# Earlier accumulator loads, GpSimd weight loads, a place for the counts and early Gelus in a graph and FFN kernel

## The chip, the cores and the metric

The kernel runs on one core of a Trainium2 chip. The metric is the device time of one launch in microseconds; of several runs the median is taken. TensorE (PE) does the matmuls, VectorE (DVE) elementwise work, ScalarE (ACT) activations and copies, GpSimd (POOL) some elementwise work and DMA issue, and SyncE (SP) only issues DMAs. Each engine works through its own instructions in a fixed order.

## The reference, cut to what matters

All data are fp32. `x` has 1250 rows (nodes) of 1024. There are 20,000 edges (`src`, `dst`).

```python
x = x + gat(LN(x))           # graph attention, 4 heads of 256
x = x + ffn(LN(x))           # 4 x 64 rails of 16, up to 64 each, gelu, then 16384 -> 1024 by w_cproj
x = x + gcn(LN(x), W, b)     # h = LN(x) @ W.T + b, weighted sum over neighbours and self
x = x + moe(LN(x))           # shared geglu + one of 8 experts by argmax
```

The change touches the end of the attention, the FFN and the GCN. The FFN is

```python
y = einsum('btri,hrij->bthrj', xr, rail_maker)
z = einsum('bthrj,hrkj->bthrk', y, rail_up_proj)
out = gelu(z.reshape(b, t, -1)) @ w_cproj.T
```

and the GCN sums `norm[:, None] * h[col]` over the rows, for which the kernel uses a matrix of edge counts between nodes.

## The kernel before, in words

**Attention.** `attend(h, b)` does one head and half of the rows: DVE makes `u` (L434), ACT its Exp (L435), DVE the weights `w` (L438), PE multiplies (L440). At the end ACT copies row sums (L444), DVE inverts them (L446, L447) and adds the result to `X` (L450). While `attend(2, 1)` and `attend(3, 1)` run, `first_half` normalizes and transposes the first five tiles of 125 rows into `xT`. Tiles 0 to 4 of `X` are stored to DRAM (`x_d`) in between, and tiles 5 to 9 after the last `attend`.

**Blocks.** The FFN's projection is a Strassen multiplication within a Strassen multiplication. The hidden columns are in 16 blocks. A block has 7 outer products of 7 inner products each: 49 steps of eight matmuls (`product`, L583). The factors X (weights, 128x512) and Y (hidden values after Gelu, 128x626) live in 33 X places and 38 Y places, which are parts of tiles named `BZ`, `arena`, `X` (its memory, once the rows have gone to DRAM) and `low`. DVE adds up factors (`add_up`, L576); `projection_plan` lists these sums with a step by which each is due, planned about 11 us ahead of its product. `load_weights` fetches weights on SP's queue (L406) as X places come free. `hidden` makes the hidden values: four matmuls of a 32-row slice (L564) and two Gelus of 626 columns (L569). For block 0 it is called at steps 0 (two pieces), 2, 3, 7, 8, 9 and 10; for later blocks in the block before.

After each product of the blocks 0 to 14, ACT copies it from PSUM (L592) to one of five staging buffers in `low`, and GpSimd issues a DMA that adds it to an accumulator in DRAM, `acc_d[p, i]` (L596), 49 in all. Products have two places in PSUM.

**Last block.** Block 15 has 7 outer products of 4 steps, each step with two pairs of factors (16 matmuls). Before it, the accumulators come back: `load_sums(p)` (L611, SP) fetches the seven of outer product p, `outer_sums(p)` is a generator of seven DVE sums (L618) that make four blocks of it. `combine` adds a product in PSUM to its block (L632) and, for the later p, adds blocks to the output in `xT` (L637). With `end` the number of the first step of the last block, `load_sums` is called for p = 1, 2, 6, 7, 4, 5, 3 at steps end-7, end, end+4, end+8, end+12, end+16, end+20. From step end-4 on, two of the waiting L618 sums are written per step, and seven at every fourth step of the last block. The rest is in the order in which the program is written; the scheduler may move an instruction in front of others on its engine where nothing forbids it.

As the last block's X places come free, the 16 GCN weight pieces (`gcn_w`, 256 KB each) are loaded into them on SP (L736), from the fifteenth of its steps in the program on (the scheduler moves them forward).

**GCN.** `linear(t)` does tile t: 16 matmuls (L762), a bias by DVE (L769), a scale by ACT. Then, in a loop over r, SP loads 125 x 1250 counts (L823, which is two DMAs by the helper at L105 and L106) into one of three buffers of a pool, GpSimd adds the identity to one part (L824), and PE multiplies: 20 matmuls of 512 columns (L828). Before this loop, SP's queue has the loads of the shared expert's weights (L794 to L796) and of the gate, which go to the memory that the linear stage leaves.

Of the kernel before, what the change touches and what calls it, by code (L numbers as in the profile page):

```python
# [8 lines left out]
F32 = mybir.dt.float32  # L9
# [4 lines left out]
AF = mybir.ActivationFunctionType  # L14
ALU = mybir.AluOpType
# [4 lines left out]
P = 128  # L20
R, T = 125, 10
N = R * T
# [75 lines left out]
def gnn_ffn_kernel(ctx, tc, x, src, dst, gat_w, a_l, a_r, maker, up, cproj,  # L98
# [4 lines left out]
    def dma(eng, out, in_):  # L103

        eng.dma_start(out[:RA], in_[:RA])  # L105
        eng.dma_start(out[RA:], in_[RA:])  # L106
# [301 lines left out]
    def rail_parts(k):  # L408
        return (spare[:, k * 464 + i:k * 464 + j] for i, j in ((0, 16), (16, 80), (80, 208), (208, 336), (336, 464)))
# [10 lines left out]
    def rails(k, pp):  # L420
# [2 lines left out]
        nc.tensor.matmul(pp, mb, ub, start=True, stop=True)  # L423
        nc.scalar.copy(pw, pp)

    with tc.tile_pool(name="att", bufs=3) as atp, tc.tile_pool(name="aps", bufs=6, space=PSUM) as aps, \
            tc.tile_pool(name="tps0", bufs=2, space=PSUM) as tps:

# [40 lines left out]
        with tc.tile_pool(name="al", bufs=2) as lnp:  # L469
            attend(2, 0)  # L470
            nc.gpsimd.memset(m8, 1.0)
            nc.gpsimd.affine_select(m8, m8, pattern=[[-16, 8]], compare_op=ALU.is_ge, fill=0.0, base=0,
                                    channel_multiplier=1)
            nc.gpsimd.affine_select(m8, m8, pattern=[[16, 8]], compare_op=ALU.is_ge, fill=0.0, base=15,
                                    channel_multiplier=-1)
            nc.vector.tensor_reduce(m2, m8.rearrange("p (a s) -> p s a", s=2), AX.X, ALU.add)
            for k in range(2):
                load_rails(0, k)
            for o in ("11", "12"):
                for i in corner:  # L480
                    load_weights(0, o, i)
            end = attend(3, 0)
            with tc.issue_after(end.ins):
                for k in range(2):
                    rails(k, tps.tile([P, 4, R], F32, name="pt").rearrange("p a b -> p (a b)")[:, :P])
            for t in range(HT):
                dma(nc.sync, x_d[t], X[:, t, :])

            def first_half():
                mv = lnp.tile([R, HT, 2], F32, name="mvh", bufs=1)  # L490
                for t in range(HT):
                    st = lnp.tile([R, 2, 6], F32, name="st")
                    for g in range(2):
                        nc.vector.bn_stats(st[:, g, :], X[:, t, g * 512:(g + 1) * 512])
                    nc.vector.bn_aggr(mv[:, t, :], st.rearrange("p a b -> p (a b)"))
                    yield
                rstd = lnp.tile([R, HT], F32, name="rstdh", bufs=1)
                nc.scalar.activation(rstd, mv[:, :, 1], AF.Sqrt, bias=eps)
                nc.vector.reciprocal(rstd, rstd)
                for t in range(HT):  # L500
                    norm[t] = lnp.tile([R, D], F32, name="xn")
                    nc.vector.tensor_scalar(norm[t], X[:, t, :], mv[:, t, 0:1], rstd[:, t:t + 1],
                                            op0=ALU.subtract, op1=ALU.mult)
                    turn(xT, norm, tps, t)
                    yield

            half = first_half()
            attend(2, 1, half)
            attend(3, 1, half)
            for t in range(HT, T):  # L510
                dma(nc.sync, x_d[t], X[:, t, :])
    rowst.close()
# [8 lines left out]

    xx = XX.rearrange("p t d -> p (t d)")
    with ExitStack() as tail:
        low = tail.enter_context(tc.tile_pool(name="lowp", bufs=1)).tile([P, T * D], F32, name="low")
        Hs = low[:R].rearrange("p (t d) -> p t d", d=D)
        accst, blocks = ExitStack(), ExitStack()
        arena = accst.enter_context(tc.tile_pool(name="accp", bufs=1)).tile([P, 33 * 512], F32, name="arena")
        rlp = blocks.enter_context(tc.tile_pool(name="rl", bufs=2))  # L530
        ops = accst.enter_context(tc.tile_pool(name="ops", bufs=2, space=PSUM))
        zps = blocks.enter_context(tc.tile_pool(name="zps", bufs=1, space=PSUM))
        two = lambda a: a.rearrange("p (q n) -> p q n", q=2)

        scratch = arena[:, 25 * 512:]
        XS += [two(arena[:, i * 512:(i + 1) * 512]) for i in range(33)]
        xw += range(8, 33)
        YS = [two(v[:, i * 2 * NQ:(i + 1) * 2 * NQ]) for v, n in ((xx, 16), (low, 16), (scratch, 6)) for i in range(n)]
        yh, parts, early = [*range(8), *range(16, 27), *range(8, 16)], list(range(27, 32)), list(range(32, 38))
        tt = nc.vector.tensor_tensor  # L540
        steps, sums = projection_plan()
        left, acc = {}, {}
# [14 lines left out]

        def hidden(b, n, k):

            pw = [*rail_parts(k)][-1]  # L560
            pz = zps.tile([P, 4, 512], F32, name="pz2")
            for q in range(4):
                rows = slice(32 * q, 32 * q + 32)
                nc.tensor.matmul(pz[:, q, :NQ], pw[rows, :], xT[rows, (2 * b + k) % KD, n * NQ:(n + 1) * NQ],  # L564
                                 start=True, stop=True)
            for i in range(2):
                key = b, "Y", f"{k + 1}{n // 2 + 1}", f"{i + 1}{n % 2 + 1}"
                buf[key] = place_y(b == NB - 1 and n > 1)
                nc.scalar.activation(view(key), pz[:, 2 * i:2 * i + 2, :NQ], AF.Gelu)  # L569
# [104 lines left out]
        def turn_tile(t):  # L674
# [4 lines left out]
        coming = {b: list(raw) for b in range(1, NB)}  # L679
        coming[0] = raw[8:]  # L680
        pieces = [(n, k) for h in range(2) for k in range(2) for n in (2 * h, 2 * h + 1)]
        first = {0: pieces[:2], 2: pieces[2:3], 3: pieces[3:4], 7: pieces[4:5], 8: pieces[5:6], 9: pieces[6:7],
                 10: pieces[7:]}
        later = dict(zip((33, 36, 38, 40, 42, 44, 46, 48), pieces))
        late = {1: 5, 2: 6, 3: 7, 4: 8, 5: 9}
        end = (NB - 1) * 49
        last, j, fill, sums_of = None, 0, [], dict(zip((end - 7, *range(end, end + 21, 4)), OUTER))
        norm = {}
        for n, (b, p, i, pairs) in enumerate(steps):
            m = n - 49 * b  # L690
# [22 lines left out]
            if b + 1 < NB:  # L713
# [4 lines left out]
                    rails(m // 2 - 14, zps.tile([P, 4, 512], F32, name="pz2")[:, 0, :P])  # L718
                if m in later:
                    hidden(b + 1, *later[m])  # L720
            assert n != end - 7 or all(v < 33 for k, v in buf.items() if k[1] == "X")
            if n in sums_of:
                load_sums(sums_of[n])
                fill.append(outer_sums(sums_of[n]))
# [5 lines left out]
            if b == NB - 1:  # L730
                if m >= 14 and len(W3) < 2 * KD:
                    for g in range(2):
                        for k in range(KD):
                            if xw and (k, g) not in W3:
                                W3[k, g] = XS[xw.pop(0)].rearrange("p q o -> p (q o)")
                                nc.sync.dma_start(W3[k, g], gcn_w[k * P:(k + 1) * P, g * 512:(g + 1) * 512])  # L736
                if m == 23:
                    nc.gpsimd.dma_start(bias, gcn_b.partition_broadcast(R))
                while m >= 16 and len(fetched) < 4 and fetch(len(fetched)):
                    pass  # L740
                if m == 22:
                    add_out(0)
                    level(0)
                if m == 24:
                    turn_tile(0)
                if m == 27:
                    add_out(1)
                    level(1)
            po = product(pairs)
            for _ in range(7 if n >= end and m % 4 == 3 else 2):  # L750
                if n > end - 5 and fill and next(fill[0], 0) == 0:
                    fill.pop(0)
            if last:
                (combine if last[0] == NB - 1 else accumulate)(*last[last[0] == NB - 1:])
# [3 lines left out]
        def linear(t):  # L758
# [10 lines left out]
            tt(Hs[:, t, :], ph.rearrange("p a b -> p (a b)"), bias, op=ALU.add)  # L769
            nc.scalar.activation(Hs[:, t, :], Hs[:, t, :], AF.Copy, scale=dis[:, t:t + 1])  # L770

        for t in range(T):
            for w in range(len(fetched), min(T, t + 5)):
                fetch(w)
            linear(t)
# [3 lines left out]

        back_end = ExitStack()  # L780
        xTp = back_end.enter_context(tc.tile_pool(name="xp3", bufs=1, side="right"))
        cp = tail.enter_context(tc.tile_pool(name="cp", bufs=3))
        psp = tail.enter_context(tc.tile_pool(name="ps3", bufs=2, space=PSUM))

        keep = back_end.enter_context(tc.tile_pool(name="xp5", bufs=1, side="right"))
# [33 lines left out]
                nc.tensor.transpose(pl[:, t0 + i, :], lgT[:, i * R:(i + 1) * R], ident[:NE, :NE])  # L819

        for r in range(T):
            cs = cp.tile([R, T, R], F32, name="cs")
            dma(nc.sync, cs, cnt_d[r])  # L823
            nc.gpsimd.tensor_tensor(cs[:, r, :], cs[:, r, :], ident[:R, :R], op=ALU.add)  # L824
            pa = psp.tile([R, 2, 512], F32, name="ph")
            for c in range(T):
                for g in range(2):
                    nc.tensor.matmul(pa[:, g, :], cs[:, c, :], Hs[:, c, g * 512:(g + 1) * 512],  # L828
                                     start=(c == 0), stop=(c == T - 1))
            if r:  # L830
                turn(xT5, norm, psp, r - 1)
                if r in (5, 9):
                    logits(r - 5, 4)
            xs = X[:, r, :]
            nc.vector.scalar_tensor_tensor(xs, pa.rearrange("p a b -> p (a b)"), dis[:, r:r + 1], xs,
                                           op0=ALU.mult, op1=ALU.add)
            normalize(norm, lnp, r)
            dma(nc.sync, xn_d[r * R:(r + 1) * R, :], norm[r])
# [218 lines left out]
```

## Time and profile before

| | |
|---|---|
| median of 3 runs | 3000.86 us (3000.56 to 3002.55) |
| the profiled execution | 3001.98 us |
| its span | 3000.2 us, so 1.8 us lie around it |
| granted PE clock, mean | 0.987 |
| PE busy | 2903.7 us (97%) |
| DVE, ACT, GpSimd busy | 1595.9, 875.9, 753.9 us |
| DMA moved | 449.57 MB, 150 GB/s over the span |
| attention's last matmul ends | 502.43 us |
| blocks 0 to 14 and the last one | until about 2336 us |
| linear stage of the GCN | about 2336 to 2490 us |
| counts rounds | about 2503 to 2706 us |

The profile page gives busy times of each engine and groups of equal instructions. The list of waits names for each engine what it stood still for: engine, tile and line that waited, an arrow, what released it, then the total, the number of times and the longest. A stretch is a window of time with busy time (and number) of each engine in it, the clock that the throttle granted PE and the share of time in which DMA engines were busy. The chain of waits goes back from the end of a stretch: start, length and what the work was. The engine names with a q (SPq) are the instruction queues that issue.

### The profile page before, as it was taken

The page shows a single profiled execution, that of the slowest core. Times are in us where ns is not written, and L with a number is a line of the kernel's source. Part 1 is how long each engine was busy: PE and PEld are TensorE (multiplying, and loading weights), DVE is VectorE, ACT ScalarE, POOL GpSimd, SP SyncE. Part 2 cuts the span into 40 slices and gives each one's busy share as a digit, 9 for nine tenths or more (in the row PEclk, how much of TensorE's full clock was granted, in tenths as well). Part 3 has the DMA queues.
Part 4 walks back from the last instruction along what each step waited for, and adds up shares of the span by engine and source line. Part 5 has one row for each costly group of instructions (what it writes and reads, how often), then busy time and mean ns, then how long its engine had stood idle before and what let it go on. Part 6 is the DMA issues. An engine that isn't in the chain of part 4 may idle for free.

```text
span 3000.2 us, 32450 instructions
## 1 busy us (share of the span) xinstructions
PE 2903.7 (97%) x11479; PEld 1915.7 (64%) x11479; DVE 1595.9 (53%) x2611; ACT 875.9 (29%) x1412; POOL 753.9 (25%) x966
## 2 busy tenths in 40 slices
PE   8999898999999999999999999999979998999998
PEld 5574776666766766766766766766657543445774
DVE  7687987746645645645655555555557321221213
ACT  1211234444344344344344334334310110000000
POOL 2010000224434434434434434434310000002001
PEclk9999999999999999999999999999989998999999
DMA  5245523569999999999999999999974003212655
GB/s 140 64 119 146 142 65 122 186 166 173 196 172 172 195 177 167 196 178 166 195 181 163 198 179 162 200 178 144 232 195 132 25 0 98 61 58 82 211 195 161
DMA packets 253572, 449.57 MB, mean 150 GB/s; under 512 B 48160, under 2 KB 132218, under 8 KB 252777
## 3 DMA queue, kind: packets, MB, share of 16 engines
q0 software_dynamic: 113936, 266.34, 51.6%
q1 hardware_dynamic: 139466, 181.05, 20.1%
q8 instruction: 96, 1.57, 0.2%
q14 instruction: 74, 0.61, 0.1%
HBM read 175.38 MB, written 271.89 MB: 149 GB/s over the span
## 4 chain that ended last, share of the span: by engine, by line
PE 83%; DMA 2%; DVE 2%; ACT 0%; issue 0%; SPq 0%; POOL 0%; DVEq 0%; POOLq 0%; ACTq 0%
PE po L583 56%; PE ph L828 6%; PE pab L859 6%; PE po L762 5%; PE pz L564 3%; PE po L440 3%; PE po L965 2%; PE po L976 1%; PE pt L153 1%; DMA X<-acc_d 1%; PE pg L814 1%; DMA cs<-cnt_d 0%; DMA yg<-ys_d,back 0%; DMA rowbd<-st 0%; PE px L668 0%; DVE y L968 0%
## 5 line engine op out<-in xcount | busy, mean ns | idle before, releaser
L583 PE MATMUL po<-X,arena 128*128 128x313 f32 x3000 | 837.1, 429 | 0.0
L596 POOL DMA_DIRECT2D acc_d<-low x686 | 593.2, 865 | 914.4 <-ACT low L592 886.3
L592 ACT COPY low<-po 128x626 f32<-128x626 f32 x735 | 500.4, 681 | 993.1 <-PE po L583 820.8
L583 PEld LDWEIGHTS po<-X,arena 128*128 128x128 f32 x3000 | 563.3, 190 | 237.1 <-issue 26.3
L583 PE MATMUL po<-low,arena 128*128 128x313 f32 x2112 | 593.9, 429 | 16.1 <-DVE arena L632 16.1
L583 PEld LDWEIGHTS po<-low,arena 128*128 128x128 f32 x2112 | 396.7, 190 | 183.3 <-issue 18.7
L576 DVE TENSOR_TENSOR arena<-arena 128x512 f32<-128x512 f32 x339 | 233.3, 691 | 84.9 <-PE po L583 80.3
L583 PE MATMUL po<-X,BZ 128*128 128x313 f32 x736 | 213.2, 432 | 4.7 <-ACT X L569 4.7
L828 PE MATMUL ph<-low,cs 125*125 125x512 f32 x400 | 176.5, 601 | 14.5 <-POOL cs L824 14.5
L583 PEld LDWEIGHTS po<-X,BZ 128*128 128x128 f32 x736 | 139.0, 191 | 64.7 <-issue 8.3
L576 DVE TENSOR_TENSOR X<-X 128x626 f32<-128x626 f32 x137 | 111.2, 814 | 100.7 <-PE po L583 100.4
L828 PEld LDWEIGHTS ph<-low,cs 125*125 125x125 f32 x400 | 75.4, 191 | 109.7 <-issue 94.4
L209 PE MATMUL pz<-W,xT 128*125 128x512 f32 x320 | 141.2, 596 | 0.1
L583 PE MATMUL po<-low,BZ 128*128 128x313 f32 x480 | 138.3, 428 | 0.0
L576 DVE TENSOR_TENSOR X<-low,X 128x626 f32<-128x626 f32 x105 | 85.2, 816 | 85.2 <-PE po L583 82.6
L576 DVE TENSOR_TENSOR low<-X 128x626 f32<-128x626 f32 x103 | 83.7, 815 | 71.6 <-PE po L583 71.3
L576 DVE TENSOR_TENSOR X<-X,low 128x626 f32<-128x626 f32 x93 | 76.0, 819 | 79.9 <-PE po L583 79.7
L277 PE MATMUL pc<-os,od 125*125 125x417 f16 (+1 forms) x588 | 110.9, 344 | 5.1 <-issue 5.1
L440 PE MATMUL po<-BZ,w 125*125 125x257 f32 x400 | 98.2, 407 | 17.0 <-DVE w L438 15.7
L583 PEld LDWEIGHTS po<-low,BZ 128*128 128x128 f32 x480 | 90.0, 190 | 36.7 <-issue 3.0
L564 PE MATMUL pz<-xT,BZ 32*128 32x313 f32 x1024 | 104.9, 479 | 4.2 <-DVE X L450 4.2
L209 PEld LDWEIGHTS pz<-W,xT 128*125 128x125 f32 x320 | 59.0, 188 | 72.9 <-issue 70.0
(235 smaller groups left out, 2904.6 us busy)
## 6 DMA issues: line engine op xcount, KB each, us to landing
acc_d<-low POOLq DMA_DIRECT2D x735, 313.0 KB, 5.8
arena<-in_cproj SPq DMA_DIRECT2D x200, 256.0 KB
w<-in_w SPq DMA_DIRECT2D x16, 1024.0 KB
BZ<-in_cproj SPq DMA_DIRECT2D x56, 256.0 KB
nm<-nm_d SPq DMA_DIRECT2D x20, 546.9 KB
w3t<-in_w SPq DMA_DIRECT2D x8, 1024.0 KB
X<-acc_d SPq DMA_DIRECT2D x19, 313.0 KB
cnt_d<-cn SPq DMA_DIRECT2D x10, 546.9 KB
```

What stands on the lines that cost most here:

```text
L209: nc.tensor.matmul(pz, xT[:, k, t * R:(t + 1) * R], W[g][:, k], start=(k == 0), stop=(k == KD - 1))
L277: nc.tensor.matmul(pc[:, b, :nn], od[:, d - near[c][0], :], os[:, n0:n0 + nn], start=(c == win[d][0]), stop=(c == win[d][-1]))
L440: nc.tensor.matmul(po[i], w[:, i * R:(i + 1) * R], Z[h // 2][:, s, h % 2, :], start=(s == 0), stop=(s == T - 1))
L564: nc.tensor.matmul(pz[:, q, :NQ], pw[rows, :], xT[rows, (2 * b + k) % KD, n * NQ:(n + 1) * NQ], start=True, stop=True)
L576: tt(view(k), *a, op=ALU.add if sign == "+" else ALU.subtract)
L583: nc.tensor.matmul(po[:, o, :NQ], view(x)[:, q, o * P:(o + 1) * P], view(y)[:, q, :], start=(i == q == 0), stop=(i + 1 == len(pairs) and q ...
L592: nc.scalar.copy(part, po[:, :, :NQ])
L596: nc.gpsimd.dma_start(out=acc_d[p - 1, i - 1], in_=part, accum_op=ALU.add)
L762: nc.tensor.matmul(ph[:, g, :], turned[t][:, k, :], W3[k, g], start=(k == 0), stop=(k == KD - 1))
L828: nc.tensor.matmul(pa[:, g, :], cs[:, c, :], Hs[:, c, g * 512:(g + 1) * 512], start=(c == 0), stop=(c == T - 1))
L859: nc.tensor.matmul(pab[:, :nn], w12[:, i, k, f * P:(f + 1) * P], rhs[:, k, n0:n0 + nn], start=(k == 0), stop=(k == KD - 1))
L965: nc.tensor.matmul(po[:m, g, :], hid[:, f, s * P:s * P + m], w3t[:, f, g * 512:(g + 1) * 512], start=(f == 0), stop=(f == 1))
```

## The change

It has four parts.

1. `load_sums` is called at end-13, end-6, end+1, end+5, end+12, end+15 and end+20, and the sums may be written from step end-8 on, nine instead of seven at every fourth step of the last block.
2. The GCN weights are loaded by GpSimd's queue instead of SP's, and not into X places 8 to 15.
3. X places 8 to 15 are a tile of their own, `first_w`, that lives until the counts are done; the arena is smaller by as much. Three counts buffers lie in it. The first three are loaded in the linear stage at t = 5, 6 and 7, and number r + 3 after the matmuls of round r. The old pool of three buffers is gone.
4. The first two pieces of hidden values of block 0 are made after `attend(3, 1)` in the program, in eight matmuls with one Gelu of 313 columns each, in the PSUM tiles of the transposes, instead of at step 0 in two calls of `hidden`. The first Y places are the same memory as before.

```diff
+    def hidden_rows(pz, b, n, k, q):
+        rows = slice(32 * q, 32 * q + 32)
+        nc.tensor.matmul(pz, [*rail_parts(k)][-1][rows, :], xT[rows, (2 * b + k) % KD, n * NQ:(n + 1) * NQ],
+                         start=True, stop=True)
...
             attend(3, 1, half)
+            for n in range(2):
+                for q in range(4):
+                    pz = tps.tile([P, 4, R], F32, name="pt").rearrange("p a b -> p (a b)")[:, :NQ]
+                    hidden_rows(pz, 0, n, 0, q)
+                    buf[0, "Y", "11", f"{q // 2 + 1}{n + 1}"] = 2 * n + q // 2
+                    nc.scalar.activation(YS[2 * n + q // 2][:, q % 2, :], pz, AF.Gelu)
...
-        arena = accst.enter_context(tc.tile_pool(name="accp", bufs=1)).tile([P, 33 * 512], F32, name="arena")
+        first_w = tail.enter_context(tc.tile_pool(name="cp", bufs=1)).tile([P, 8 * 512], F32, name="first_w")
+        arena = accst.enter_context(tc.tile_pool(name="accp", bufs=1)).tile([P, 25 * 512], F32, name="arena")
...
-        first = {0: pieces[:2], 2: pieces[2:3], 3: pieces[3:4], 7: pieces[4:5], 8: pieces[5:6], 9: pieces[6:7],
+        first = {2: pieces[2:3], 3: pieces[3:4], 7: pieces[4:5], 8: pieces[5:6], 9: pieces[6:7],
...
-        last, j, fill, sums_of = None, 0, [], dict(zip((end - 7, *range(end, end + 21, 4)), OUTER))
+        last, j, fill, sums_of = None, 0, [], dict(zip((end + v for v in (-13, -6, 1, 5, 12, 15, 20)), OUTER))
...
-                            if xw and (k, g) not in W3:
-                                W3[k, g] = XS[xw.pop(0)].rearrange("p q o -> p (q o)")
-                                nc.sync.dma_start(W3[k, g], gcn_w[k * P:(k + 1) * P, g * 512:(g + 1) * 512])
+                            at = [v for v in xw if not 8 <= v < 16]
+                            if at and (k, g) not in W3:
+                                xw.remove(at[0])
+                                W3[k, g] = XS[at[0]].rearrange("p q o -> p (q o)")
+                                nc.gpsimd.dma_start(W3[k, g], gcn_w[k * P:(k + 1) * P, g * 512:(g + 1) * 512])
...
-            for _ in range(7 if n >= end and m % 4 == 3 else 2):
-                if n > end - 5 and fill and next(fill[0], 0) == 0:
+            for _ in range(9 if n >= end and m % 4 == 3 else 2):
+                if n > end - 9 and fill and next(fill[0], 0) == 0:
...
+        def counts(r):
+            return first_w[:R, r % 3 * N:r % 3 * N + N].rearrange("p (t j) -> p t j", j=R)
+        def load_counts(r):
+            dma(nc.sync, counts(r), cnt_d[r])
+            nc.gpsimd.tensor_tensor(counts(r)[:, r, :], counts(r)[:, r, :], ident[:R, :R], op=ALU.add)
         for t in range(T):
+            if 5 <= t < 8:
+                load_counts(t - 5)
...
-            cs = cp.tile([R, T, R], F32, name="cs")
-            dma(nc.sync, cs, cnt_d[r])
-            nc.gpsimd.tensor_tensor(cs[:, r, :], cs[:, r, :], ident[:R, :R], op=ALU.add)
+            cs = counts(r)
...
+            if r + 3 < T:
+                load_counts(r + 3)
```

More of the change, by code (lines that the diff above doesn't have):

```diff
@@ L424, in rails @@
         nc.scalar.copy(pw, pp)
+    def hidden_rows(pz, b, n, k, q):
+        rows = slice(32 * q, 32 * q + 32)
+        nc.tensor.matmul(pz, [*rail_parts(k)][-1][rows, :], xT[rows, (2 * b + k) % KD, n * NQ:(n + 1) * NQ],
+                         start=True, stop=True)
+    YS = [XX.rearrange("p t d -> p (t d)")[:, i * 2 * NQ:(i + 1) * 2 * NQ].rearrange("p (q n) -> p q n", q=2) for i in range(16)]
     with tc.tile_pool(name="att", bufs=3) as atp, tc.tile_pool(name="aps", bufs=6, space=PSUM) as aps, \
@@ L517, in gnn_ffn_kernel @@
                         zero[0:1].to_broadcast([1, D // 128, 128]))
-    xx = XX.rearrange("p t d -> p (t d)")
     with ExitStack() as tail:
@@ L533, in gnn_ffn_kernel @@
         two = lambda a: a.rearrange("p (q n) -> p q n", q=2)
-        scratch = arena[:, 25 * 512:]
-        XS += [two(arena[:, i * 512:(i + 1) * 512]) for i in range(33)]
+        scratch = arena[:, 17 * 512:]
+        XS += [two(v[:, i * 512:(i + 1) * 512]) for v, n in ((first_w, 8), (arena, 25)) for i in range(n)]
         xw += range(8, 33)
-        YS = [two(v[:, i * 2 * NQ:(i + 1) * 2 * NQ]) for v, n in ((xx, 16), (low, 16), (scratch, 6)) for i in range(n)]
-        yh, parts, early = [*range(8), *range(16, 27), *range(8, 16)], list(range(27, 32)), list(range(32, 38))
+        YS += [two(v[:, i * 2 * NQ:(i + 1) * 2 * NQ]) for v, n in ((low, 16), (scratch, 6)) for i in range(n)]
+        yh, parts, early = [*range(4, 8), *range(16, 27), *range(8, 16)], list(range(27, 32)), list(range(32, 38))
         tt = nc.vector.tensor_tensor
@@ L558, in hidden @@
         def hidden(b, n, k):
-            pw = [*rail_parts(k)][-1]
             pz = zps.tile([P, 4, 512], F32, name="pz2")
             for q in range(4):
-                rows = slice(32 * q, 32 * q + 32)
-                nc.tensor.matmul(pz[:, q, :NQ], pw[rows, :], xT[rows, (2 * b + k) % KD, n * NQ:(n + 1) * NQ],
-                                 start=True, stop=True)
+                hidden_rows(pz[:, q, :NQ], b, n, k, q)
             for i in range(2):
@@ L720, in gnn_ffn_kernel @@
                     hidden(b + 1, *later[m])
-            assert n != end - 7 or all(v < 33 for k, v in buf.items() if k[1] == "X")
+            assert n != end - 13 or all(v < 33 for k, v in buf.items() if k[1] == "X")
             if n in sums_of:
@@ L781, in gnn_ffn_kernel @@
         xTp = back_end.enter_context(tc.tile_pool(name="xp3", bufs=1, side="right"))
-        cp = tail.enter_context(tc.tile_pool(name="cp", bufs=3))
         psp = tail.enter_context(tc.tile_pool(name="ps3", bufs=2, space=PSUM))
```

## The prediction

> **What bounds the kernel now.** I read the page's busy shares first, then the list of what TensorE (PE) waited for, then the stretches around the largest of those waits, and last the chain of work in each stretch. PE is busy for 2903.7 us of a span of 3000.2, so at most 96.5 us of standing still can be taken back, and this change takes no arithmetic away. The list of PE's waits gives the total, the number and the longest:
>
> ```profile
> PE po L583 <- DVE arena L632: 16.1, 1, 16.1
> PE ph L828 <- POOL cs L824: 14.5, 1, 14.5
> ...
> PE po L583 <- ACT X L569: 4.7, 1, 4.7
> PE pz L564 <- DVE X L450: 4.2, 1, 4.2
> ```
>
> Four single waits, 39.5 us, stand at three places: the step from the attention to the blocks (two of them), the start of the last block, and the first counts round. The stretches (length, PE busy, PEld, DVE, ACT, POOL, granted PE clock, DMA share, GB/s) show what each place is short of:
>
> ```profile
> 502.00:517.00 15.00, 6.14 (x23) 2.75 (x23) 14.54 (x35) 8.20 (x13) 0.00 (x0) 0.61 0.81 267
> ...
> 2187.00:2207.00 20.00, 19.12 (x82) 12.55 (x80) 6.02 (x9) 7.24 (x10) 4.32 (x5) 1.00 1.07 263
> 2207.00:2222.00 15.00, 0.00 (x0) 0.00 (x0) 10.33 (x14) 0.00 (x0) 0.00 (x0) 0.55 0.70 231
> ...
> 2489.00:2503.00 14.00, 0.00 (x0) 0.00 (x0) 0.86 (x2) 1.15 (x1) 1.46 (x7) 0.60 1.02 283
> ```
>
> In the first PE is idle 8.86 us. In the next two the DMA engines are full while PE still works and not full once it stands, so order counts there and not bytes alone. In the last nothing but DMA works. The chain at the start of the last block (start, length, what):
>
> ```profile
> 2195.85 0.88 SPq L736
> ...
> 2196.82 9.63 DMA X<-acc_d
> ...
> 2209.90 5.49 DMA X<-acc_d
> ...
> 2217.10 2.70 DMA X<-acc_d
> ...
> 2221.40 0.81 DVE arena L632
> 2222.22 0.04 issue
> 2222.26 2.98 PE po L583 x5
> ```
>
> PE's last work before it is done at 2206.1. Then three loads of accumulators follow each other, each held by a buffer or by the queue before it: a GCN weight load (L736) stood in front of the first. The first combine (L632) is behind 21 sums (L618) in DVE's order. At the counts:
>
> ```profile
> 2490.91 11.59 DMA cs<-cnt_d
> 2502.49 0.07 issue
> 2502.56 0.46 POOL cs L824
> ```
>
> The load was issued only at 2490.91, because SP stood 147.2 us at the third shared weight load (L796), which waits for the linear stage to end. Each stop is also paid a second time at a low clock. The counts' matmuls alone:
>
> ```profile
> 2503.00:2521.00 18.00, 17.93 (x35) 7.76 (x36) 0.84 0.14 33
> 2525.00:2543.00 18.00, 17.31 (x42) 7.42 (x41) 1.00 0.25 82
> ```
>
> At full clock one takes 17.31/42 = 0.412 us, so 35 need 14.4 and not 17.93: 3.5 us lost.
>
> **What the Trainium skill says.** *TensorE: Matmul & The Clock Gate*, "What's actually happening": after an idle window of about 3.4 us the array runs at half rate until it has been busy for as long. The trace agrees: 0.60 and 0.61 of the clock in the stops, and the lost 3.5 us. *ScalarE: Activation LUTs*, "What ACT_TABLE_LOAD costs": about 1.28 us for the load and 1.38 us of drain. Here loads take 1.283 us, and the Gelu at 511.97 follows its load of 510.68 at once, so I use 1.28. *DMA: Bandwidth & Descriptors*, "Issuing engines are not separate DMA queues": loads from another engine run on the same 16 DMA engines and save only issue time. The share of 1.07 before the last block agrees that there is nothing spare, so I give the move to GpSimd no bandwidth.
>
> **A. First Gelus in the attention.** Removed: two groups of four matmuls (pz, L564; 1.43 us of chain for the first at the low clock, 1.35 for the second) and four Gelus (0.69 us each) between the attention and the products, with the table loads between them. Added: eight single matmuls, eight Gelus of half the width, and two table loads. A half Gelu is not in the trace: above 0.69/2 = 0.35, below 0.69; I take 0.40. By the order of instructions in the changed program, one Gelu with a table load on either side (1.28 + 0.40 + 1.28 = 2.96 us) lies on ACT before the last four Exps. ACT was idle 6.9 us for DVE in 480 to 502, so it fits, but the load of the Exp table comes after the wait for DVE's u: the Exp is up to 1.28 us later. The other seven follow the row sums' copies, which end at about 502.6. A product may start after the fifth of these and after DVE's L450 (over at 506.46): 502.6 + 1.28 + 5 x 0.40 = 505.9, so about 506.5 instead of 512.72. That is 6.2 us, and the second pz group adds 1.35. I take off 1.28 for the Exp: 6.3, rounded to 6. The first slow products stay slow. Hiding lost: if the Exp and the five longest Gelus (0.69) both count in full, 5. The third product needs a sum that DVE's order now has right after the attention; if weights that are loaded from 502.5 on are late instead, the gain falls to 1. Bounds 1 and 8.
>
> **B. Sums earlier, weights on GpSimd.** The loads of outer product 1 are asked for 6 steps sooner, those of 2 six, of 6 and 7 three; two of product 4 also come forward. SP loses 16 issues of about 0.37 us and the 12.5 us it stood at L736; GpSimd gains 16, taken at the 0.865 us of its accumulates (12.95 us busy in the 37 before 2187, so it has room). DVE's order has now 24 sums before the first combine instead of 21; the two last need acc[6,3] and acc[7,3]. The load of acc[6,3] goes to the staging buffer of the last accumulate but one. The ACT copy into that is the one at 2194.71, done at 2195.40; issue 0.86; landing 7.2 (median of 12 there): 2203.5. The load's issue 0.4 and its landing, 2.70 to 5.49 by the chain: 2206.6 to 2209.4. Two sums and the combine at 0.81: 2209.0 to 2211.8. The new bytes in front, two loads of 313 KB at 263 GB/s, 2.4 us: 2211.4 to 2214.2. I take 2214, since DVE itself has about twelve sums (9.7 us) left when the loads of 7 begin to land, about 2201 by the same lengths. Gain 2222.26 - 2214 = 8. The stop is then still 8 us, so its slow clock remains. The weight loads are no new bytes (13 were issued by SP in 2150 to 2240), but they now stand between accumulates. Five staging buffers, one per 2.2 us, allow 11 us; landing takes 4.9 to 8.2, so 3 to 6 us hide it. Past that ACT cannot copy and PE stands in block 14. Bounds: 14 (DVE ready when the last load lands early) and -5 (no gain, and the cover overrun by that).
>
> **C. Counts in their own place.** Three counts loads are asked for at t = 5, 6 and 7 of the linear stage, past the shared weights on SP, where DMA is at 0.04; their GpSimd adds go too. The first counts matmul then waits only for DVE's L769 of the last tile: 1.24 + 0.05 us after the linear's last matmul, so 1.3 instead of 14.5: 13.2. A stop of 1.3 us is far below what slowed the clock at the other places (4.2 and up), so the 3.5 us go as well: 16.7. I take 16, for tiles that ACT is still scaling. The later loads start after a round of 18 us and have two rounds; 11.59 us would do. The shared weights are issued when they were, and PE first uses them at 2706. If the slow clock stays, 12. The eight buffers are kept from the GCN weights, so some of the 16 weights come later; all wait on products of the last block that are 40 us or more ahead of the linear stage. I cost it at nothing; if a weight is late, a few us. Bounds 9 and 17.
>
> **Sum.** 6 + 8 + 16 = 30. The profiled execution took 3001.98 us (1.8 around its span): 2972. The median is 1.1 lower than it: 2971.
>
> **Rivals.** (1) The change does not do what it says at B: with 24 sums ahead and full DMA engines the last landing is where it was. For it: 1.07 DMA share, and more sums ahead. Against: the share of 0.70 in the stop, the queueing at L736 that goes. 2971 + 8 = 2979; with a late weight at A, 2984. (2) All cover holds: the loads land early and DVE is through at 2208, A gives its 8: 2971 - 6 - 2 = 2963. For it: load landings of 2.70 when the engines are free. (3) Slower than before. GpSimd works in order, and the first moved weight loads wait for a DVE sum that itself stands behind a sum waiting for an accumulator load (9.63 us here). If that happens twice, the accumulates behind are 19 us late, and eight weight loads at one accumulate's step of 2.2 us add 17.6; less the 3 us of cover, PE stands 34 us in the last steps of block 14, against A and C's 22 with B gone: about 3012. It decides once the accumulates are held more than 25 us. Against: the first weight loads depend on sums that come before the sums of product 6, and DVE's 9.4 us wait in this profile cost PE nothing in block 14.
>
> **How the numbers follow.** Likeliest case 2971, from 2965 to 2976: 0.52. Rival 1: 0.24. Rival 2: 0.16. Rival 3 and the like: 0.04. Within 0.2% (about what a measurement of this kernel can tell from no change; 2995 to 3007): 0.04, when B overruns and C's gain is eaten by late weights. The range 2961 to 2985 takes in rivals 1 and 2 and leaves 0.15 out. Faster 0.92, same 0.04, slower 0.04.
>
> **What would show it.** A: first product at about 506.5, no L564 wait after the attention. B: PE back at about 2214, with the first combine (L643 after the change) its releaser; new ACT or DVE waits between 2150 and 2206 would mean rival 3. C: the wait before the first counts matmul near 1.3 us at full clock. A late weight for the linear stage, or a wait at the third product, would break A or C.

## The result and the profile after

The changed kernel takes 2979.01 us (median of 4 runs, 2978.19 to 2980.72) where the one before takes 3001.05 beside it: a ratio of 0.9926, 95% interval 0.9909 to 0.9944. It is faster by 22.0 us; 2971 was forecast, with 2961 to 2985 as the range. The profiled execution's span is 2976.5 us, 23.7 less than before.

PE's list of waits, after:

```profile
PE po L594 <- DVE arena L643: 14.4, 1, 14.4
...
PE pt L428 <- ACT X L523: 1.7, 3, 1.3
...
PE ph L848 <- issue: 1.4, 1, 1.4
```

The first line is the last block, the second the early Gelus, the last the counts. So of the four waits that were shown before, the counts' 14.5 has shrunk to 1.4 and the Gelus' 4.7 and 4.2 to 1.7, and the one at the start of the last block has only fallen from 16.1 to 14.4. The stretches (length, PE busy, PEld, DVE, ACT, POOL, granted clock, DMA share, GB/s) say the same:

```profile
502.00:517.00 15.00, 13.34 (x46) 8.54 (x46) 10.84 (x23) 7.59 (x17) 0.63 (x2) 0.89 0.72 233
2187.00:2202.00 15.00, 14.66 (x59) 9.47 (x58) 5.56 (x8) 4.50 (x6) 10.14 (x14) 1.00 1.00 253
2202.00:2216.00 14.00, 0.00 (x0) 0.00 (x0) 9.52 (x13) 0.00 (x0) 0.00 (x0) 0.65 0.85 247
...
2485.00:2503.00 18.00, 17.92 (x42) 7.96 (x43) 0.55 (x2) 1.15 (x1) 1.02 (x6) 1.00 0.51 167
```

After the attention PE works 13.34 of 15 us and not 6.14. The first 18 us of the counts hold 42 matmuls at full clock and not 35 at 0.84: 7 x 0.412 = 2.9 us. The stop at the last block is still there nearly whole, at a clock of 0.65.

Where the 23.7 us come from, by the times at which PE passes the same places:

| place | before | after | gained up to here |
|---|---|---|---|
| first product starts | 512.72 | 509.69 | 3.0 |
| PE stops at the last block | 2206.1 | 2201.8 | 4.3 |
| PE goes on | 2222.26 | 2216.24 | 6.0 |
| first counts matmul | 2503.07 | 2485.08 | 18.0 |
| first shared expert matmul | 2706.4 | 2685.6 | 20.8 |
| end of the span | 3000.2 | 2976.5 | 23.7 |

The attention's end is worth 4.3 (the second group of pz matmuls, which stood between the halves of the first product, went too). The last block's stop is worth 1.7. Between it and the counts 12.0 are gained: 13.2 of the counts' stop less 1.2 lost in the last block and the linear stage. Then 2.8 follow, the clock's 2.9. The last 2.9 come in the experts, which the change does not touch; the profiles do not say what they are, and runs of one kernel differ by as much (in part why the two profiles lie 23.7 apart and the medians 22.0).

### The profile page after: what moved, and what is told of

It reads as the page before. It is cut to its first block, busy times and chain, and to the rows that moved or that the text cites. A ratio compares the mean times of both kernels' runs of the same rounds, so it can differ in the third digit from the quotient of the medians.

```text
span 2976.5 us, 32458 instructions
## 1 busy us (share of the span) xinstructions
PE 2900.6 (97%) x11479; PEld 1914.0 (64%) x11479; DVE 1595.5 (54%) x2611; ACT 874.9 (29%) x1415; POOL 764.3 (26%) x982
## 5 line engine op out<-in xcount | busy, mean ns | idle before, releaser
L594 PE MATMUL po<-X,arena 128*128 128x313 f32 x2176 | 613.7, 429 | 0.1
L594 PEld LDWEIGHTS po<-X,arena 128*128 128x128 f32 x2176 | 408.3, 190 | 173.4 <-issue 19.9
L594 PE MATMUL po<-low,arena 128*128 128x313 f32 x1552 | 440.2, 429 | 14.4 <-DVE arena L643 14.4
L594 PEld LDWEIGHTS po<-low,arena 128*128 128x128 f32 x1552 | 291.4, 190 | 137.0 <-DVE arena L643 14.9
L594 PE MATMUL po<-X,first_w 128*128 128x313 f32 x840 | 240.0, 428 | 0.0
L594 PEld LDWEIGHTS po<-X,first_w 128*128 128x128 f32 x840 | 157.6, 189 | 66.5 <-issue 6.8
L848 PE MATMUL ph<-low,first_w 125*125 125x512 f32 x400 | 173.6, 593 | 1.4 <-issue 1.4
L594 PE MATMUL po<-low,first_w 128*128 128x313 f32 x560 | 160.6, 429 | 0.0
L848 PEld LDWEIGHTS ph<-low,first_w 125*125 125x125 f32 x400 | 74.2, 188 | 94.8 <-issue 94.8
L594 PEld LDWEIGHTS po<-low,first_w 128*128 128x128 f32 x560 | 104.6, 190 | 44.2 <-issue 5.5
```

Source lines behind the costliest of these rows:

```text
L594: nc.tensor.matmul(po[:, o, :NQ], view(x)[:, q, o * P:(o + 1) * P], view(y)[:, q, :], start=(i == q == 0), stop=(i + 1 == len(pairs) and q ...
```

## What the two traces say of the last block

These are instructions in the order of time (start, length, engine, line, operation, in brackets the idle time before it and what ended it). DVE before its first combine (L643):

```profile
2200.59 1.66 DVE L629 TENSOR_TENSOR X<-X 128x626 f32<-128x626 f32 x2 [8.58 <-DMA X<-acc_d]
...
2214.66 0.81 DVE L629 TENSOR_TENSOR X<-X 128x626 f32<-128x626 f32 x1
2215.38 0.80 DVE L643 TENSOR_TENSOR arena<-po,arena 128x626 f32<-128x626 f32 x1
```

DVE waits 8.58 us for an accumulator of product 7 and does sums of 7 and 6 until 2215, all ahead of the first combine. In all 25 sums stand ahead of it in this trace and 22 in the one before; the prediction counted 24 and 21. ACT and GpSimd in the same trace:

```profile
2177.55 0.68 ACT L603 COPY low<-po 128x626 f32<-128x626 f32 x1 [1.05 <-issue]
...
2186.40 0.58 POOL L749 DMA_DIRECT2D arena<-in_gcn_w  x1 [10.06 <-DVE arena L587]
2186.97 0.90 POOL L607 DMA_DIRECT2D acc_d<-low  x1
...
2194.74 0.68 ACT L603 COPY low<-po 128x626 f32<-128x626 f32 x1 [0.53 <-DMA acc_d<-low]
...
2199.78 0.87 POOL L607 DMA_DIRECT2D acc_d<-low  x1 [2.57 <-DMA arena<-in_gcn_w]
```

The product copied at 2177.55 is accumulated only at 2186.97, because a GCN weight load stands ahead of it for 10.06 us for a sum of DVE. The last copy is done at 2195.42, and its accumulate is issued at 2199.78, 2.57 us of that waiting for an earlier weight load to land. ACT waited 4.3 us for staging buffers.

There are two theories of the stop. **Theory T:** the weight loads on GpSimd hold the accumulates up, and so the accumulator loads. **Theory D:** the order of DVE makes the stop. The first combine needs the seven sums of product 1 and nothing else, but it stands behind sums of 2, 7 and 6 whose loads land last. The rival of both is that the DMA engines are full and the last byte decides.

## The experiments

The kernel before, beside them, took 2998.1 to 3006.9 us. Runs of one kernel spread over 1.5 to 11 us, so medians that differ by under 2 us are called equal, and the wait in the trace decides. "The stop" is PE's wait for the combines at the last block.

**e1_w3_late.** The weight loads behind the last accumulate on GpSimd's queue.

```diff
-                                nc.gpsimd.dma_start(W3[k, g], gcn_w[...])
+                                with tc.issue_after(acc["last"].ins):
+                                    nc.gpsimd.dma_start(W3[k, g], gcn_w[...])
```

> The changed kernel, but all 16 GCN weight loads stand on GpSimd's queue behind the last accumulate of block 14 instead of between the accumulates. Theory T (the moved weight loads hold the accumulates up: one of them stands 10.06 us for a DVE sum, and the last accumulate is issued 4.4 us after its copy, 2.6 of it for an earlier weight load): the accumulates go out at once again, the last about 4 us sooner and the ones before up to 8.5 sooner, PE's stop at the last block falls from 14.4 us to 7 to 10, the time from 2979 to 2973 to 2975. Rival R (the DMA engines are full, so the same bytes end at the same time; or DVE's 24 sums ahead of the first combine set it): the stop stays at 13 to 15, the time within 1 us of 2979.

Measured: 2980.65 us, ratio 0.9931 (0.9918 to 0.9945); stop 16.3. Theory T fails as the cause of the stop. In its trace the accumulates do run free, and yet:

```profile
2196.15 0.86 POOL L607 DMA_DIRECT2D acc_d<-low  x1 [2.18 <-ACT low L603]
...
2198.86 1.54 SPq L622 DMA_DIRECT2D X<-acc_d  x3
...
2208.22 1.66 DVE L629 TENSOR_TENSOR X<-X 128x626 f32<-128x626 f32 x2 [8.68 <-DMA X<-acc_d]
...
2219.00 0.80 DVE L643 TENSOR_TENSOR arena<-po,arena 128x626 f32<-128x626 f32 x1
```

The last accumulate goes out right after its copy. DVE waits for the same accumulator of 7 as before, now until 2208. Its load is itself late: three loads go out from 2198.86 on, where the changed kernel has them at 2191.3 to 2192.8, because SP waits for places that five sums of product 2 free, and these sums stood 6.20 us for an accumulator (0.75 in the changed kernel). The loads then run beside eight weight loads that GpSimd issues from 2196.7 on. How the delay divides between the two is not shown.

**e2_w3_sp.** The weight loads back on SP: `nc.sync.dma_start(W3[k, g], ...)` for `nc.gpsimd.dma_start(W3[k, g], ...)`.

> The changed kernel, but the GCN weight loads on SP's queue as before the change. Theory T: accumulates free, but SP's accumulator loads again stand behind weight loads that wait (12.5 us in the kernel before), so part of the gain only: stop 9 to 14, 2974 to 2978. Rival R: no difference from 2979. If SP's queue was what held the kernel before and GpSimd's is no cost, it is slower than 2979 by 2 or more.

Measured: 2979.49 us, 0.9932 (0.9918 to 0.9945); stop 12.9. The stop is 1.5 shorter, the time equal: which queue issues them is worth nothing that can be measured in this kernel.

**e3_old_sums.** Part 1 alone undone.

```diff
-dict(zip((end + v for v in (-13, -6, 1, 5, 12, 15, 20)), OUTER))
+dict(zip((end - 7, *range(end, end + 21, 4)), OUTER))
-for _ in range(9 if n >= end and m % 4 == 3 else 2):
-    if n > end - 9 and fill ...
+for _ in range(7 if n >= end and m % 4 == 3 else 2):
+    if n > end - 5 and fill ...
```

> The changed kernel with the loads of the accumulators and the sums at the steps of before (end-7, end, end+4 and so on; two sums from end-4, seven at every fourth step). Theory T: DVE no longer stands up to 16 us for early accumulator loads in block 14, so the first weight load is not held by DVE and the accumulates run free, but the sums come late: stop 14 to 18, 2979 to 2982. Rival R (earlier sums are what gained the 1.7 us at this place): stop 16 or more, 2981 and up.

Measured: 2979.34 us, 0.9926 (0.9913 to 0.9940); stop 16.1. The time is that of the changed kernel: the earlier loads by themselves brought nothing. Parts 1 and 2 were undone one at a time, not together.

**e4_gelu_back.** Part 4 alone undone: the loop of eight `hidden_rows` removed, `first = {0: pieces[:2], ...}` again.

> The changed kernel with the first Gelu pieces back at step 0 of block 0, four matmuls and two Gelus of 626 columns each, as before. By the traces the early Gelus are worth 4.3 us (PE reaches the stop at the last block at 2201.8 instead of 2206.1): 2983 to 2984. If the last block's stop is set by transfers that do not move with PE, less: 2979 to 2981.

Measured: 2987.26 us, 0.9954 (0.9940 to 0.9967): 8 us slower than the changed kernel, where 4.3 come out of the two profiles. In its trace the waits of 4.7 and 4.2 us are back, the first product starts 10.7 us after the attention's last matmul starts instead of 5.7, and the stop is 15.4, 1.0 longer. Part 4 is worth 4 to 8 us; the spread of the runs does not allow more.

**e5_order_first.** The sums of 6 and 7 behind the first combine in DVE's order.

```diff
-                tt(YS[a[d]], YS[a[x]], YS[a[y]], op=op)
+                if p in (6, 7):
+                    with tc.issue_after(first_combine[0].ins):
+                        tt(YS[a[d]], YS[a[x]], YS[a[y]], op=op)
+                else:
+                    tt(YS[a[d]], YS[a[x]], YS[a[y]], op=op)
...
             po = product(pairs)
+            if last and last[0] == NB - 1:
+                combine(*last[1:])
...
-            if last:
-                (combine if last[0] == NB - 1 else accumulate)(*last[last[0] == NB - 1:])
+            if last and last[0] < NB - 1:
+                accumulate(*last)
```

> The changed kernel, with the sums of outer products 6 and 7 put behind the first combine in DVE's order, and the combine written ahead of the step's sums: the first combine follows 14 sums instead of 24, all of products 1 and 2. Nothing else is changed; loads and GpSimd's queue stay. Theory D (what ends the stop is DVE's order: the first combine needs only the sums of product 1, but waits behind sums of 7 and 6 whose loads land at 2200 to 2211): DVE reaches the first combine by 2200, but the second and third still stand behind sums of 6, so PE's stop falls from 14.4 us to 0 to 8, and the time from 2979 to 2964 to 2973. Rival R (the combine's own data or full DMA engines hold it): the stop stays at 13 or more and the time at 2978 or more.

Measured: 2978.38 us, 0.9919 (0.9906 to 0.9933), no gain, against the expectation of D. But the stop moved, and it is 9.8 us instead of 14.4; a new wait of 3.5 us in block 14 takes most of the difference:

```profile
2154.86 0.81 DVE L633 TENSOR_TENSOR low<-arena,low 128x626 f32<-128x626 f32 x1 [21.37 <-DMA low<-acc_d]
...
2157.98 3.18 PE L594 MATMUL po<-X,first_w 128*128 128x313 f32 x8 [3.52 <-DVE first_w L587]
...
2202.38 0.81 DVE L649 TENSOR_TENSOR arena<-po,arena 128x626 f32<-128x626 f32 x1 [8.30 <-PE po L594]
...
2217.56 0.81 DVE L631 TENSOR_TENSOR low<-low 128x626 f32<-128x626 f32 x1 [8.71 <-DMA low<-acc_d]
...
2219.72 0.81 DVE L649 TENSOR_TENSOR arena<-po,arena 128x626 f32<-128x626 f32 x1
```

The first combine (L649 here) now waits for PE and not PE for it. The second stands behind sums of 6, one of which waits until 2217.56 for an accumulator. The wait in block 14 is a price of the earlier loads (part 1): DVE stands there for an accumulator ahead of a factor that PE needs, 21.37 us here and 15.99 in the changed kernel, where PE was still covered.

**e6_order_all.** The same for every sum, behind the latest combine, and none in the first three steps.

```diff
+                if combines:
+                    with tc.issue_after(combines[-1].ins):
...
-                if n > end - 9 and fill ...
+                if n > end - 9 and not end <= n < end + 3 and fill ...
```

> As the run before, with no sums written in the first three steps of the last block and every later sum behind the latest combine: the first three combines follow each other with no sum between. Theory D: PE does not stop at the last block, or under 2 us, and the low clock after the stop goes too: 14.4 and about 2 less, 2962 to 2966. It must not come back later: if the sums of 6 are then late for their combines, waits of L594 for DVE turn up between 2210 and 2250 and part of it is lost. Rival R: 2978 or more.

Measured: 2970.93 us, 0.9898 (0.9882 to 0.9913), 8 us less than the changed kernel, but not 2962 to 2966; stop 7.2, now at the fourth combine:

```profile
2196.75 0.81 DVE L649 TENSOR_TENSOR arena<-po,arena 128x626 f32<-128x626 f32 x1 [5.95 <-PE po L594]
...
2215.47 0.81 DVE L631 TENSOR_TENSOR low<-low 128x626 f32<-128x626 f32 x1 [9.47 <-DMA low<-acc_d]
...
2219.93 0.80 DVE L649 TENSOR_TENSOR arena<-po,arena 128x626 f32<-128x626 f32 x1
```

The order is the cause of half of the stop here. What is left waits for acc[6,2], which the program puts into the staging buffer of the very last accumulate.

**e9_order_late.** e6 with the weight loads behind the last accumulate, as in e1.

> Run e6_order_all with the GCN weight loads behind the last accumulate of block 14 on GpSimd. With DVE's order out of the way, what is left of the stop there (7.2 us) ends on the load of acc[6,2], which goes into the staging buffer of the very last accumulate. Theory H (weight loads between the accumulates hold that accumulate up): it is issued about 4 us sooner, and the stop falls to 2 to 4 us: 2966 to 2969. Rival (the weight loads then collide with the accumulator loads themselves, as in e1_w3_late): stop 7 or more, 2971 or more.

Measured: 2968.04 us, 0.9884 (0.9867 to 0.9900); stop 3.2. Here, with DVE's order out of the way, theory T's mechanism costs what it said, 4 us of stop; the medians are 2.9 apart, and the intervals of the two ratios overlap.

**e10_order_place.** e6 with another order of the loads of product 6.

```diff
-            for i in (2, 3, 4, 5, 1, 6, 7):
+            for i in (3, 4, 5, 2, 1, 6, 7) if p == 6 else (2, 3, 4, 5, 1, 6, 7):
```

> Run e6_order_all with the loads of product 6 in the order 3, 4, 5, 2, 1, 6, 7 instead of 2, 3, 4, 5, 1, 6, 7: part 2, which the first sum of 6 needs, takes the staging buffer of an earlier accumulate, and part 3, which the last but one needs, that of the last. Theory: the wait of DVE for the load of acc[6,2] (9.5 us) shrinks by two accumulates' spacing, 4 to 5 us, but 3 is needed before combine four, so the stop falls from 7.2 to 3 to 6: 2967 to 2970. Rival (all these loads land together at the end, held by the accumulates): stop 7, no difference from 2971.

Measured: 2963.38 us, 0.9871 (0.9855 to 0.9888); stop 0.5. This is the fastest kernel, 15.6 us below the changed one by the medians, and 38.9 below the kernel before beside it. Its stretches at the same place:

```profile
2187.00:2202.00 15.00, 15.00 (x63) 10.35 (x62) 2.62 (x4) 4.23 (x6) 6.52 (x9) 1.00 1.05 284
2202.00:2216.00 14.00, 13.51 (x51) 9.40 (x51) 8.88 (x12) 0.00 (x0) 1.62 (x3) 1.00 0.78 253
```

PE works through at full clock where the changed kernel stands at 0.65.

**e11_order_late_place.** Both at once.

> Both at once: weight loads behind the last accumulate, and the places of product 6 in the other order. If both hold, the stop is under 3 us and the time 2964 to 2968, the fastest of all; if the loads collide with the weights, as for e9_order_late.

Measured: 2963.97 us, 0.9875 (0.9859 to 0.9892); no stop. Equal to e10: there was 0.5 us left to take, and with the other order of the loads the place of the weight loads has no price.

**e12_before_order.** The kernel before, with DVE's order alone changed: the edit of e6, but with the sums left out at step `end` only.

> The kernel before, with DVE's order alone changed at the last block: the combine is written ahead of the step's sums, and every sum written after the first combine stands behind the latest one. The first combine then follows the seven sums of product 1 and none of 2 or 6. Loads, their steps, the GCN weights on SP, the counts and the Gelus are as before. Theory D (the order made the stop, not the lead of the loads): PE's stop of 16.1 us falls to 0 to 6 us, and with its low clock the time from 3001 to 2984 to 2991. Rival (the earlier loads of the change are needed for it, since acc[2,1] and its like land only at 2206 and later): the stop only moves to the second to fifth combine, 8 us or more are left, 2993 or more.

Measured: 2983.86 us, 0.9942 (0.9928 to 0.9956), 17.5 us below the kernel before, and the stop of 16.1 us is gone, with the counts' stop (14.4) and the Gelus' (4.7 and 4.2) still there. The same stretch in it:

```profile
2187.00:2206.00 19.00, 19.00 (x87) 12.35 (x86) 4.52 (x7) 9.20 (x13) 5.59 (x7) 1.00 1.08 278
2206.00:2222.00 16.00, 16.00 (x61) 11.30 (x61) 12.30 (x18) 0.00 (x0) 0.00 (x0) 1.00 1.01 354
```

This settles it: with the steps at which the loads are written and the queue of the weights as they were, changing DVE's order alone takes the stop away. Part of the effect goes by way of SP: it stood 12.5 us for DVE ahead of its weight loads in the kernel before and stands 3.0 here, and three accumulator loads that went out at 2193.96 to 2196.82 go out at 2188.45 to 2191.51. The DMA engines carry 354 GB/s beside working PE, where they moved 231 at a share of 0.70 while it stood, so they were not what held it. That no stop is left here and 7.2 us are left in e6 does not speak for the old loads: the first combine comes at 2205.23 here and at 2196.75 there, so the loads have 8.5 us more.

**e7_counts_late.** The counts' first three loads written just ahead of their loop.

```diff
-            if 5 <= t < 8:
-                load_counts(t - 5)
...
+        for r in range(3):
+            load_counts(r)
         for r in range(T):
```

> The changed kernel with the counts still in their own place, but the first three loads and adds written just ahead of the counts' loop, behind the shared weights on SP, and not at t = 5 to 7 of the linear stage. If the time of asking is what took the stop away, a stop of 12 to 15 us comes back before the first counts matmul, with about 3 us at a low clock: 2993 to 2997. If the own place alone does it, because the scheduler moves the loads forward, no difference from 2979.

Measured: 2981.53 us, 0.9939 (0.9925 to 0.9952), from 2976.73 to 2988.0; no stop at the counts. The median is 2.5 above the changed kernel's, inside a spread of 11.3. SP's loads of the first three counts in this kernel:

```profile
L105 SPq DMA_DIRECT2D first_w<-cnt_d x3: 304/340/345, 2329.1 to 2335.5; - x3
```

They start from 2329.1 to 2335.5, as they do in the changed kernel (2330.7 to 2337.1), although they are written after the linear stage. The place of their own is what took the stop away; the step at which they are written is worth nothing, since the scheduler moves them to where the place is free (the last products that read `first_w` are under way at 2330).

**e8_gelu_mid.** The order of e6, and the loop of eight early Gelus moved ahead of `attend(3, 1, half)`.

> The order of run e6_order_all, and the eight early Gelus written between the last two attention calls instead of behind them. ACT then has them between Exps, with three pairs of table loads (5.1 us more of loads) instead of one, and the eight matmuls lie under the attention. Theory: after the attention's last matmul PE waits only for the row sums and DVE's L458, about 4 us, instead of the 5.3 us in which it alternates with ACT over two PSUM tiles, so 1 to 3 us less than e6_order_all. Rival: the Exps come later by the table loads and the attention ends as much later: 1 to 4 us more than e6_order_all.

Measured: 2974.89 us, 0.9906 (0.9891 to 0.9922): 4 us more than e6. Six table loads of 1.283 us stand between Exps, and the attention's last matmul starts at 511.1 where it starts at 502.7 in e6. The rival was right.

## Why the prediction was right, and where a step failed

The sum was 6 + 8 + 16 = 30; the median fell by 22.0. Direction and range held. The likeliest case, 2965 to 2976, did not come: 2979 is the time of rival 1, which the range took in. One term was wrong.

**C, 16.** The stop of 14.5 became 1.36 (1.3 was forecast), 13.2 us as forecast, and the clock gave 2.9 where 3.5 was taken. The mechanism was right, that the first matmul then waits for the last tile only. The half clock after an idle window, which the Trainium skill states (*TensorE: Matmul & The Clock Gate*, "What's actually happening"), agrees with the traces on both sides: after 14.5 us the longest counts matmul takes 1.217 us where the median is 0.593, and the clock is 0.84 over the first 18 us; after 1.36 us the longest takes 0.665, at a clock of 1.00. The reason given for it, that the loads are asked for at t = 5 to 7 of the linear stage, is not what counts: they go out at 2330.7 to 2337.1, ahead of that stage, because the place is free, whatever the step at which they are written (e7).

**A, 6.** Measured 4.3 in the profiles and 8 by e4's median. From the start of the attention's last matmul to the first product it is 5.0 (10.7 to 5.7), and the second pz group adds 1.3: 6.3, the size that was forecast. The profiles show 4.3 because the attention ends 1.9 later in the one after. The working was off within it: the first product starts at 509.69, not at 506.5. The Gelus were taken to follow each other at 0.40 us. They take 0.43 but come in pairs every 1.31 us, because eight matmuls share two PSUM tiles and PE runs at the low clock:

```profile
504.57 1.28 ACT L523 ACT_TABLE_LOAD   x1
...
506.35 1.11 PE L428 MATMUL pt<-xT,BZ 32*128 32x313 f32 x4 [1.27 <-ACT X L523]
...
508.97 0.79 PE L428 MATMUL pt<-xT,BZ 32*128 32x313 f32 x2 [0.20 <-ACT X L523]
...
509.69 2.89 PE L594 MATMUL po<-X,BZ 128*128 128x313 f32 x5
```

The attention's later end is no larger than the spread of runs: its last matmul starts at 501.5 to 504.8 in the ten kernels with the Gelus behind the attention, and at 500.9, 502.0 and 505.2 in the three that keep them at step 0. The 1.28 taken off for the Exp's table load can't be seen in it.

**B, 8.** This is the step that failed: measured 1.7. The forecast took the load of acc[6,3] as the last thing and set two sums and the combine behind it, 2214. It had the start of product 7's loads (2201) and twelve sums of DVE as a second bound, and by adding A's 6 to B's 8 it let both move with PE's earlier arrival. What happened is the second bound, and nothing moved: the load of 7 landed at 2200.6, as estimated, and thirteen vector operations with 4.1 us of waits for loads between them took until the combine at 2215.4, while PE arrived 4.3 us sooner than before. What the working never asked is whether those sums belong ahead of the first combine. They don't, as e6 and e12 show; the 24 sums were read as a fact of the kernel and not as the cost. Rival 1 named two reasons for a gain of nothing at B: the sums ahead and full DMA engines. The first was right, the second was not: in e12 loads pass at 354 GB/s with no stop. That its time, 2979, was met to the microsecond is luck, since B gave 1.7 and the experts 2.9 that no term forecast.

**Weight loads on GpSimd, 0.** In time it is 0 (e2). But the cover of "3 to 6 us" was overrun: accumulates went out 8.5 us late and ACT waited 4.3 us, of which PE felt nothing that its list of waits shows. Rival 3's first half was there, a weight load 10.06 us behind a DVE sum, without its price. The loads cost 4 us of stop only once DVE's order is mended (e6 against e9), and nothing once product 6 is loaded in the other order too (e10 against e11).

Of the change, then, the place for the counts and the early Gelus make up the gain, and the earlier sums and the move of the weights make up nothing that can be measured when each is undone alone. The gain that was looked for at the last block did not go into a new wait: it was never in the lead of the loads.

## What to carry to other kernels

When an engine with a fixed order feeds the bottleneck, list what stands ahead of the first instruction that the bottleneck waits for, and ask of each item whether that instruction needs it; asking for its data sooner gained 1.7 us here, putting it behind took away a stop of 16.1. When several things are late at one place, take the one that ends last away first: the second (the weight loads between the accumulates) showed no price until then. And where a scheduler places the loads, give the load a place that is free early; the line at which it is written may not matter.

## What the runs showed of the hardware

The same busy share of the DMA engines can go with very different GB/s: 263 at a share of 1.07 in the kernel before (2187 to 2207), 354 at 1.01 in e12 (2206 to 2222). The queues (packets, MB, share of the 16 engines) show why. The first two lines are the kernel before, where q0 is GpSimd's accumulates and q1 SP's loads; the third is e12; the last is e1 from 2203 to 2212, when its accumulates are over and q0 is GpSimd's weight loads:

```profile
q0 software_dynamic: 1013, 2.25, 62.1%
q1 hardware_dynamic: 1469, 2.98, 44.3%
...
q1 hardware_dynamic: 2636, 5.33, 90.2%
...
q0 software_dynamic: 423, 1.36, 40.4%
```

Share times 16 engines times the length of the stretch, divided by the MB, gives an estimate of the engines' time per MB: 88 us for the accumulates, and 48, 43 and 43 for the three groups of loads. So an accumulated byte held the engines about 1.9 times as long as a loaded one beside it, and the lower GB/s was no room left over.

An accumulate on GpSimd's queue waited 2.57 us, by its releaser in the trace, for an unrelated weight load on the same queue to land (2.31 in e5, 2.42 in e6). One that was issued after 2190 in the changed kernel took 12.5 us to land; in e1, with no weight load among them, the last three took 5.5 to 6.0.
